# Fetching operand tiles as gathers by row number from a transposed table in DRAM

## Chip, cores and metric

The kernel runs on one core of a Trainium2 chip. The metric is the device time of one execution in microseconds (us); the median of three runs before is 1005.7 us.

## What is computed

A compressed interaction network over x of shape (1024, 39, 64), float32, in three layers with 64 outputs each. Each layer forms all products of its input's rows with the rows of x, and contracts them with a weight matrix:

```python
def _cin_layer(Xk, X0, W, b):
    O = W.shape[0]
    Hk, Fdim = (Xk.shape[1], X0.shape[1])
    Wr = W.reshape(O, Hk, Fdim)
    return jnp.einsum('bhe,bfe,ohf->boe', Xk, X0, Wr) + b[None, :, None]
X0 = sparse_embedding
Xk = X0
outs = []
for W, b in ((W0, b0), (W1, b1), (W2, b2)):
    Xk = _cin_layer(Xk, X0, W, b)
    outs.append(Xk.sum(axis=-1))
cin_output = jnp.concatenate(outs, axis=-1)
return cin_output @ fc_w.T + fc_b
```

## The kernel before

Only products x[f] * x[g] of two rows of x are needed: the last layer is folded into the weights, and the outputs of the first layer are multiplied with a second linear form of the same products. Every unordered pair (f, g) of the 39 rows (fields) is formed once. The 65536 columns (batch times 64) are worked off in 32 blocks of 2048 columns (BLK), so that one row of a block is 8 KB.

**Operand tiles.** For a block n, the tile r[n] holds four operands of 128 partitions by 2048 columns. Operand i holds 39 fields three times, each time rotated by a different amount (BASE, STEP), on 117 partitions, and 11 more rows (EXTRA) on the rest; operand 0 has ones there instead. The six pairs of operands (PAIRS) give six products of 128 rows (chunks 0 to 5). The seventh chunk holds what is left and needs only half of the partitions: the tiles u and v hold two blocks at once, the even one on partitions 0 to 63, the odd one on 64 to 127. There are two buffers of r (rt), two of u and two of v.

**How the tiles are filled.** load (L113) brings a block of x, transposed to fields by columns in pieces of 256 bytes, into an SBUF stage tile xs. store (L119) writes that twice into a DRAM tile xd of 78 rows, so that a rotation is one run of rows. roll (L124) then reads each operand back with one copy of 117 rows from xd (L127), and the 11 extra rows of operands 1 to 3 with one more (L128). roll_half (L132) fills the half tiles with five copies (L139). In the steady loop operands 0 and 1 are issued on SP's queue and 2 and 3 on POOL's; L128, store and roll_half are on SP's, load is on POOL's.

**The weights.** Before the loop, W0 and the folded W1, W2 are written into two DRAM tables (wide0, wide), and gathered (L227) in the row order of the chunks into wa and wb; POOL issues the gathers from wide0, ACT and SP those from wide. DVE adds wb to wa, one chunk at a time, in the first block (L356).

**The loop.** The order is written out by hand. steps lists (block, chunk); an even block has seven chunks, an odd one six. DVE forms the product of four steps ahead (product, L277 and L279) into one of four buffers p. TensorE multiplies it with wa (multiply, L294, and L305 for the half chunk), into two PSUM tiles a block. After the first chunk of a block, finish for the block before runs: ACT L325, DVE L329 and L333; and fields copies 39 rows of u (ACT L318). When the loop comes to chunk 0 of block n it issues roll(n+1), and then roll_half(n+2), store(n+3) and load(n+4).

Of the kernel before, what the change touches and what calls it, by code (L numbers as in the profile page):

```python
# [45 lines left out]

F32 = mybir.dt.float32  # L50
AF = mybir.ActivationFunctionType
ALU = mybir.AluOpType
AX = mybir.AxisListType

B, F, E, H = 1024, 39, 64, 64
FH = F * H
NG = 3
K = NG * F
STEP = (0, 15, 9, 6)
BASE = (0, 3, 5, 20)  # L60
LAST = 11
EXTRA = (None, 6, 17, 28)
NX = 11
HR = 64
# [5 lines left out]
BLK = 2048  # L70
BB = BLK // E
SB = SUB // E
NBLK = B // BB
FW = 2 * F
FX = FW + 2

_dist = sorted(
    min(d % F, -d % F)
# [9 lines left out]
def rows(t, first, steps, n):  # L88

    base = t[:]  # L90
    width = base.ap[-1][1] if len(base.ap) == 2 else n
    ap = [[s * width, k] for s, k in steps] + [[1, n]]
    return bass.AP(base.tensor, base.offset + first * width, ap)
# [3 lines left out]
def cin_kernel(ctx: ExitStack, tc: tile.TileContext, x, w0t, b0, w1, b1, w2, b2, fc_w, fc_b, out):  # L97
    nc = tc.nc
    PSUM = bass.MemoryType.PSUM
    DRAM = bass.MemoryType.DRAM  # L100

    const = ctx.enter_context(tc.tile_pool(name="const", bufs=1))
    dram = ctx.enter_context(tc.tile_pool(name="dram", bufs=1, space=DRAM))
    xds = ctx.enter_context(tc.tile_pool(name="xds", bufs=5, space=DRAM))
    stage = ctx.enter_context(tc.tile_pool(name="stage", bufs=3))
    prods = ctx.enter_context(tc.tile_pool(name="prods", bufs=4))
    psum = ctx.enter_context(tc.tile_pool(name="psum", bufs=4, space=PSUM))
    ctx.enter_context(tc.manual_schedule())

    xv = x.rearrange("b f e -> f b e")  # L110
    xs, xd, r = {}, {}, {}

    def load(n, engine):  # L113
        xs[n] = stage.tile([F, BLK], F32, name="xs", tag="xs")
        engine.dma_start(  # L115
            xs[n].rearrange("p (b e) -> p b e", e=E), xv[:, n * BB : (n + 1) * BB, :]
        )

    def store(n):  # L119
        xd[n] = xds.tile([FW, BLK], F32, name="xd", tag="xd")  # L120
        nc.sync.dma_start(xd[n][0:F], xs[n])
        nc.sync.dma_start(xd[n][F:FW], xs[n])

    def roll(n, engines):  # L124
        r[n] = rt[n % 2]
        for i in range(4):
            engines[i].dma_start(r[n][0:K, i], rows(xd[n], BASE[i], [(1, F), (STEP[i], NG)], BLK))  # L127
        nc.sync.dma_start(  # L128
            r[n][K:128, 1:4], rows(xd[n], EXTRA[1], [(1, NX), (LAST, 3)], BLK)
        )  # L130

    def roll_half(n):  # L132
        h = n % 2 * HR
        for t, pieces in (
            (ut, ((0, 56, 0), (56, 62, 28))),
            (vt, ((0, F, 0), (45, 56, 34), (56, 62, F))),
        ):
            for p0, p1, first in pieces:
                nc.sync.dma_start(  # L139
                    t[n // 2 % 2][h + p0 : h + p1], xd[n][first : first + p1 - p0]  # L140
                )

    wa = const.tile([128, NCHUNK, 2 * H], F32, name="wa")
    wb = const.tile([128, NCHUNK, 2 * H], F32, name="wb")
    fc = const.tile([H, 3], F32, name="fc")
    fc2 = const.tile([H, 32], F32, name="fc2")
    v2 = const.tile([H, FX], F32, name="v2")
    bias = const.tile([H, 2], F32, name="bias")
# [2 lines left out]
    wfin = const.tile([H + F, 1], F32, name="wfin")  # L151
    kfin = const.tile([1, 1], F32, name="kfin")

    rt = [const.tile([128, 4, BLK], F32, name=f"r{k}") for k in range(2)]
    ut = [const.tile([128, BLK], F32, name=f"u{k}") for k in range(2)]
    vt = [const.tile([128, BLK], F32, name=f"v{k}") for k in range(2)]
# [6 lines left out]
    prep = tc.tile_pool(name="prep", bufs=1)  # L163
    with prep as prep:

        w2s = prep.tile([H, FH], F32, name="w2s")
        w1s = prep.tile([H, FH], F32, name="w1s")
        nc.sync.dma_start(w2s, w2)
        nc.scalar.dma_start(fc, fc_w.rearrange("o (l h) -> h (o l)", h=H))
        nc.scalar.dma_start(w1s, w1)  # L170
        load(0, nc.sync)
        w0v = w0t.rearrange("b a h -> b (a h)")
        for i in range(2):
            for k in range(2):
                engine = nc.scalar if i else nc.gpsimd
                engine.dma_start(wide0v[i * F : (i + 1) * F, k * F * H : (k + 1) * F * H], w0v)
        nc.scalar.dma_start(bias[:, 0:1], b1.rearrange("(h o) -> h o", o=1))
        nc.scalar.dma_start(bias[:, 1:2], b2.rearrange("(h o) -> h o", o=1))
        nc.scalar.dma_start(b0s[H:128], b0.rearrange("(h o) -> h o", o=1))
        nc.scalar.dma_start(fcb, fc_b.rearrange("(p o) -> p o", o=1))  # L180
        for k in range(2):
            nc.gpsimd.memset(rt[k][96:128, 0], 1.0)
            nc.gpsimd.memset(ut[k], 1.0)
            nc.gpsimd.memset(vt[k], 1.0)
        store(0)
        roll(0, [nc.sync] * 4)
        roll_half(0)

        nc.vector.memset(wa, 0.0)
        nc.vector.memset(wb, 0.0)  # L190
        nc.vector.memset(wfin[0:H], 1.0)
        nc.vector.tensor_copy(fc2, fc[:, 2:3].to_broadcast([H, 32]))
        nc.vector.tensor_copy(v2[:, FW:FX], fc[:, 1:2].to_broadcast([H, 2]))  # L193


        n8 = 8 * F
        pv = psum.tile([128, 2, MM], F32, name="pv", tag="po")
        vrow = prep.tile([128, 2, n8], F32, name="vrow")
        for half in range(2):
            for t in range(4):  # L200
                g = 4 * half + t
                nc.tensor.matmul(  # L202
                    pv[32 * t : 32 * t + 32, half, 0:n8],
                    fc2,
                    w2s[:, g * n8 : (g + 1) * n8],
                    start=True,
                    stop=True,
                )
            nc.vector.tensor_copy(vrow[:, half], pv[:, half, 0:n8])
            nc.scalar.dma_start(v2[32 * half : 32 * half + 32, 0:F], vrow[0:128:32, half])  # L210
        nc.vector.tensor_copy(v2[:, F:FW], v2[:, 0:F])  # L211


        w1v = w1s.rearrange("o (h f) -> o f h", f=F)
        for g in range(5):
            f0, f1 = 8 * g, min(8 * g + 8, F)
            n = (f1 - f0) * H
            pt = psum.tile([128, SUB], F32, name="pt", tag="po")
            nc.tensor.matmul(pt[0:FX, :n], v2, w1v[:, f0:f1, :], start=True, stop=True)  # L219
            part = prep.tile([FX, MM], F32, name=f"part{g}")  # L220
            nc.vector.tensor_copy(part[:, :n], pt[0:FX, :n])  # L221
            for k in range(2):
                nc.scalar.dma_start(widev[:, (k * F + f0) * H : (k * F + f1) * H], part[:, :n])
# [23 lines left out]
        main(nc.gpsimd, wa[:, c], wide0, i, k, w0cols)  # L247
        main(nc.gpsimd, wb[:, c], wide0, k, i, w0cols)
    rest(nc.gpsimd, nc.gpsimd, wide0, w0cols)
    load(1, nc.gpsimd)  # L250
    load(2, nc.gpsimd)
    gather(nc.sync, wa[K:128, 0:3, tcols], wide, FW * FW + EXTRA[1], (1, NX), (LAST, 3))
    for c, (i, k) in enumerate(PAIRS):
        main(nc.scalar, wa[:, c], wide, i, k, tcols)
        main(nc.sync if c % 2 else nc.scalar, wb[:, c], wide, k, i, tcols)
    gather(nc.sync, wa[F:45, NPAIR, tcols], wide, FW * FW, (1, 6))
    rest(nc.sync, nc.scalar, wide, tcols)
    store(1)
    roll_half(1)


    pc = psum.tile([128, SUB], F32, name="pc", tag="po")
# [3 lines left out]
    nc.scalar.copy(wfin[H : H + F], pc[0:F, 0:1])  # L266
    nc.scalar.activation(kfin, pc[0:1, MM : MM + 1], AF.Identity, bias=fcb, scale=float(E))

# [52 lines left out]
    def finish(n):  # L321
        x1 = []
        for h in range(BLK // SUB):
            t = work.tile([H, SUB], F32, name="x1", tag="x1")
            nc.scalar.activation(t, po[n][h][H:128, :], AF.Identity, bias=b0s[H:128])  # L325
            x1.append(t)
# [14 lines left out]
    p = {s: product(*s) for s in steps[:AHEAD]}  # L341
    for at, (n, c) in enumerate(steps):
        if c == 0:
            if n + 1 < NBLK:
                roll(n + 1, [nc.sync, nc.sync, nc.gpsimd, nc.gpsimd])
            for k in (2, 3) if n == 0 else (n + 3,):
                if n > 0 and n + 2 < NBLK:
                    roll_half(n + 2)
                if k < NBLK:
                    store(k)  # L350
                if k + 1 < NBLK:
                    load(k + 1, nc.gpsimd)
            if n == 0:
                roll_half(2)
        if n == 0:
            nc.vector.tensor_tensor(wa[:, c], wa[:, c], wb[:, c], ALU.add)  # L356
            if c == NPAIR:
                nc.scalar.copy(wa[HR : 2 * HR, c], wa[0:HR, c])  # L358
        multiply(n, c, p.pop((n, c)))
        if c == 0:  # L360
            if n > 0:
                finish(n - 1)
            fields(n)
        if at + AHEAD < len(steps):
            p[steps[at + AHEAD]] = product(*steps[at + AHEAD])
# [3 lines left out]
    for m in range(B // MM):  # L369
        py = psum.tile([128, SUB], F32, name="py", tag="po")  # L370
        nc.tensor.matmul(py[0:1, 0:MM], wfin, sums[:, bass.ts(m, MM)], start=True, stop=True)  # L371
        nc.scalar.activation(y[:, bass.ts(m, MM)], py[0:1, 0:MM], AF.Identity, bias=kfin)
    nc.sync.dma_start(out.rearrange("b o -> o b"), y)
# [42 lines left out]
```

## Time and profile before

| what | value |
|---|---|
| runs before, us | 996.43, 1005.7, 1010.02 |
| profiled execution, us | 992.35 |
| its span from first to last instruction, us | 990.2 |
| DMA traffic, MB | 198.58 |
| HBM read, written, MB | 176.12, 23.61 |
| ACT busy, us | 141.1 |
| POOL busy, us | 90.4 |

The busy times are sums over the span, which holds a start (the weights, some 60 us), the loop, and an end. The DMA share is the mean busy share of the core's 16 DMA engines. Ends of matmuls are modelled in the trace, so a busy TensorE need not be at its full pace.

### The profile page before, as it was taken

The page shows a single profiled execution, that of the slowest core. Times are in us where ns is not written, and L with a number is a line of the kernel's source. Part 1 is how long each engine was busy: PE and PEld are TensorE (multiplying, and loading weights), DVE is VectorE, ACT ScalarE, POOL GpSimd, SP SyncE. Part 2 cuts the span into 40 slices and gives each one's busy share as a digit, 9 for nine tenths or more (in the row PEclk, how much of TensorE's full clock was granted, in tenths as well). Part 3 has the DMA queues.
Part 4 walks back from the last instruction along what each step waited for, and adds up shares of the span by engine and source line. Part 5 has one row for each costly group of instructions (what it writes and reads, how often), then busy time and mean ns, then how long its engine had stood idle before and what let it go on. Part 6 is the DMA issues. An engine that isn't in the chain of part 4 may idle for free.

```text
span 990.2 us, 5329 instructions
## 1 busy us (share of the span) xinstructions
PE 787.0 (79%) x1828; PEld 335.2 (34%) x1828; DVE 624.3 (63%) x356; ACT 141.1 (14%) x134; POOL 90.4 (9%) x124
## 2 busy tenths in 40 slices
PE   1334599789688799695978999786969969598997
PEld 0011244334233243242433434332424324243442
DVE  1151386587766485784765778765849577395794
ACT  0010021102111111010111021110211101021112
POOL 7210000000000000010000000000000000000000
PEclk9997799989898989797999899898988979799999
DMA  7749889889898889798888879888888988889830
GB/s 194 236 105 203 215 209 213 217 208 229 214 208 210 194 217 204 208 212 214 215 202 211 211 228 218 229 222 212 224 211 213 194 194 215 225 205 204 197 85 0
DMA packets 37658, 198.58 MB, mean 201 GB/s; under 512 B 11633, under 2 KB 11828, under 8 KB 15043
## 3 DMA queue, kind: packets, MB, share of 16 engines
q1 hardware_dynamic: 20633, 124.39, 50.8%
q0 software_dynamic: 14128, 70.55, 30.6%
q10 hardware_dynamic: 2870, 3.30, 1.1%
q8 instruction: 14, 0.23, 0.1%
q14 instruction: 13, 0.11, 0.0%
HBM read 176.12 MB, written 23.61 MB: 202 GB/s over the span
## 4 chain that ended last, share of the span: by engine, by line
DMA 86%; PE 7%; DVE 2%; SPq 1%; issue 1%; ACTq 1%; ACT 0%; DVEq 0%
DMA r<-xd 45%; DMA xd<-xs 18%; DMA u<-xd 18%; PE po L294 6%; DVE p L277 2%; DMA wide<-part 2%; DMA xs<-in_x 1%; DMA v<-vrow 1%; ACTq L227 1%; DMA wa<-wide 1%; SPq L227 0%; SPq L139 0%; PE po L305 0%; SPq L127 0%; DVE g L329 0%
## 5 line engine op out<-in xcount | busy, mean ns | idle before, releaser
L294 PE MATMUL po<-p,wa 128*128 128x512 f32 x1536 | 712.7, 626 | 172.3 <-DVE p L277 120.2
L277 DVE TENSOR_TENSOR p<-r 128x2048 f32<-128x2048 f32 x192 | 428.8, 2285 | 313.6 <-DMA r<-xd 238.8
L294 PEld LDWEIGHTS po<-p,wa 128*128 128x128 f32 x1536 | 306.3, 201 | 577.8 <-issue 410.4
L325 ACT ACTIVATE x<-po,b0s 64x1024 f32<-64x1024 f32 x64 | 71.1, 1111 | 349.5 <-PE po L305 194.9
L318 ACT COPY g<-u 39x1024 f32<-39x1024 f32 x64 | 66.6, 1043 | 377.1 <-DVE sums L333 377.1
L127 POOL DMA_DIRECT2D r<-xd x62 | 36.0, 581 | 828.7 <-DVE p L277 708.3
L329 DVE SCALAR_TENSOR_TENSOR g<-po,fc,x 64x1024 f32<-64x1024 f32 x64 | 81.2, 1269 | 8.4 <-ACT x L325 8.4
L333 DVE TENSOR_REDUCE sums<-g 103x16 f32<-103x1024 f32 x64 | 78.1, 1220 | 2.2
L305 PE MATMUL po<-p,wa 64*128 64x512 f32 x256 | 61.1, 615 | 2.6 <-DVE wa L356 2.6
L279 DVE TENSOR_TENSOR p<-u,v 128x2048 f32<-128x2048 f32 x16 | 36.6, 2284 | 8.2 <-DMA v<-xd 8.2
L305 PEld LDWEIGHTS po<-p,wa 64*128 64x128 f32 x256 | 25.8, 192 | 36.8 <-issue 32.4
L115 POOL DMA_DIRECT2D xs<-in_x x31 | 31.2, 1007 | 1.9 <-issue 1.6
L219 PE MATMUL pt<-w1s,v 64*80 64x512 f32 (+1 forms) x10 | 9.5, 1109 | 13.0 <-DVE v L211 13.0
L202 PE MATMUL pv<-w2s,fc 64*32 64x312 f32 x16 | 2.5, 724 | 8.6 <-DVE v L193 8.0
L358 ACT COPY wa<-wa 64x128 f32<-64x128 f32 x1 | 0.3, 296 | 61.9 <-DVE wa L356 61.9
L266 ACT ACT_TABLE_LOAD x1 | 1.3, 1283 | 54.3 <-DMA wb<-wide 54.3
L219 PEld LDWEIGHTS pt<-w1s,v 64*80 64x80 f32 x10 | 2.2, 230 | 19.8 <-DVE v L211 14.1
L211 DVE COPY v<-v 64x39 f32<-64x39 f32 x1 | 0.2, 176 | 12.2 <-DMA v<-vrow 12.2
L221 DVE COPY part<-pt 80x512 f32<-80x512 f32 (+1 forms) x5 | 3.4, 673 | 6.8 <-PE pt L219 6.8
L227 POOL DMA_DIRECT2D wa<-wide x10 | 6.5, 650 | 4.9 <-DMA wb<-wide 2.8
L227 POOL DMA_DIRECT2D wb<-wide x9 | 6.0, 672 | 2.2 <-DMA wb<-wide 2.2
L371 PE MATMUL py<-sums,wfin 103*1 103x512 f32 x4 | 2.2, 620 | 3.7 <-DVE sums L333 3.7
(26 smaller groups left out, 22.5 us busy)
## 6 DMA issues: line engine op xcount, KB each, us to landing
r<-xd SPq DMA_DIRECT2D x66, 936.0 KB
r<-xd POOLq DMA_DIRECT2D x62, 936.0 KB, 20.0
xd<-xs SPq DMA_DIRECT2D x64, 312.0 KB
u<-xd SPq DMA_DIRECT2D x32, 448.0 KB
v<-xd SPq DMA_DIRECT2D x32, 312.0 KB
xs<-in_x POOLq DMA_DIRECT2D x31, 312.0 KB, 25.7
r<-xd SPq DMA_DIRECT2D x32, 264.0 KB
v<-xd SPq DMA_DIRECT2D x32, 88.0 KB
```

The lines of the kernel that those rows point to most:

```text
L115: engine.dma_start(xs[n].rearrange("p (b e) -> p b e", e=E), xv[:, n * BB : (n + 1) * BB, :])
L127: engines[i].dma_start(r[n][0:K, i], rows(xd[n], BASE[i], [(1, F), (STEP[i], NG)], BLK))
L219: nc.tensor.matmul(pt[0:FX, :n], v2, w1v[:, f0:f1, :], start=True, stop=True)
L227: engine.dma_start(dst, rows(table, first, steps, H))
L277: nc.vector.tensor_tensor(p, r[n][:, i], r[n][:, k], ALU.mult)
L279: nc.vector.tensor_tensor(p, ut[n // 2 % 2], vt[n // 2 % 2], ALU.mult)
L294: nc.tensor.matmul(po[n][m // 2][:, at], wa[:, c, :], p[:, bass.ts(m, MM)], start=(c == 0 and first), stop=(c == NPAIR - 1 and not first),)
L305: nc.tensor.matmul(po[n + h][m // 2][:, at], wa[w, c, :], p[w, bass.ts(m, MM)], start=(h == 1), stop=(h == 0),)
L318: nc.scalar.copy(gt[H : H + F], ut[n // 2 % 2][h : h + F, bass.ts(m, SUB)])
L325: nc.scalar.activation(t, po[n][h][H:128, :], AF.Identity, bias=b0s[H:128])
L329: nc.vector.scalar_tensor_tensor(gt[0:H], po[n][h][0:H, :], fc[:, 0:1], x1[h], ALU.add, ALU.mult)
L333: nc.vector.tensor_reduce(sums[:, b_at : b_at + SB], gt.rearrange("p (b e) -> p b e", e=E), AX.X, ALU.add)
```

## The change

The stage tile, the DRAM tile of 78 rows and the copies of roll and roll_half go. Three DRAM tables of 80 rows of 8 KB (xd0 to xd2) hold two blocks each: rows 0 to 38 and 40 to 78 are the fields, rows 39 and 79 are ones. load writes a block of x into its table directly, from DRAM to DRAM, on SP's queue and four blocks ahead. Ten lists of 128 row numbers are made at the start by POOL (iota) and DVE, written to DRAM and read back transposed into an SBUF tile (lists, 128 by 10). Each operand tile is one indirect DMA on POOL's queue: 128 rows of 8 KB, row p taken from the table by the number in partition p of the list. A block needs four of them; u and v of a pair of blocks need one each. Copied rows include the ones and, in u and v, padding. The six memsets of rt, ut and vt go.

```diff
-    xds = ctx.enter_context(tc.tile_pool(name="xds", bufs=5, space=DRAM))
-    stage = ctx.enter_context(tc.tile_pool(name="stage", bufs=3))
...
+    xd = [dram.tile([2 * FT, BLK], F32, name=f"xd{k}") for k in range(NTAB)]
+
+    def load(n):
+        first = n % 2 * FT
+        nc.sync.dma_start(
+            xd[n // 2 % NTAB][first : first + F].rearrange("f (b e) -> f b e", e=E),
+            xv[:, n * BB : (n + 1) * BB, :],
         )
...
-    def roll(n, engines):
+    def gather_rows(dst, n, k):
+        table = xd[n // 2 % NTAB][: FT if k < 4 else 2 * FT]
+        nc.gpsimd.indirect_dma_start(
+            dst, None, table, bass.IndirectOffsetOnAxis(ap=lists[:, k : k + 1], axis=0)
+        )
+
+    def roll(n):
         r[n] = rt[n % 2]
         for i in range(4):
-            engines[i].dma_start(r[n][0:K, i], rows(xd[n], BASE[i], [(1, F), (STEP[i], NG)], BLK))
-        nc.sync.dma_start(
-            r[n][K:128, 1:4], rows(xd[n], EXTRA[1], [(1, NX), (LAST, 3)], BLK)
-        )
+            gather_rows(r[n][:, i], n, n % 2 * 4 + i)
 
     def roll_half(n):
...
+        gather_rows(ut[n // 2 % 2], n, 8)
+        gather_rows(vt[n // 2 % 2], n, 9)
...
+        nc.vector.memset(row, 0)
+        for i in range(4):
+            nc.gpsimd.iota(
+                row[:, i, 0:K], pattern=[[1, F], [STEP[i], NG]], base=BASE[i], channel_multiplier=0
+            )
+            if i:
+                ramp(i, K, NX, EXTRA[i])
...
+        nc.vector.tensor_scalar(wrap, row, F, -F, ALU.is_ge, ALU.mult)
+        nc.vector.tensor_tensor(row, row, wrap, ALU.add)
...
+        ones = prep.tile([2, BLK], F32, name="ones")
+        nc.vector.memset(ones, 1.0)
...
-        load(0, nc.sync)
+        load(0)
+        nc.sync.dma_start(rowd, row)
+        nc.sync.dma_start(lists, rowd.rearrange("k p -> p k"), allow_slow_non_contiguous=True)
+        for k in range(NTAB):
+            nc.sync.dma_start(xd[k][F : 2 * FT : FT], ones)
+        load(1)
...
-        for k in range(2):
-            nc.gpsimd.memset(rt[k][96:128, 0], 1.0)
-            nc.gpsimd.memset(ut[k], 1.0)
-            nc.gpsimd.memset(vt[k], 1.0)
-        store(0)
-        roll(0, [nc.sync] * 4)
-        roll_half(0)
+        roll(0)
...
     rest(nc.gpsimd, nc.gpsimd, wide0, w0cols)
-    load(1, nc.gpsimd)
-    load(2, nc.gpsimd)
+    roll_half(0)
...
     rest(nc.sync, nc.scalar, wide, tcols)
-    store(1)
-    roll_half(1)
+    load(2)
+    load(3)
...
             if n + 1 < NBLK:
-                roll(n + 1, [nc.sync, nc.sync, nc.gpsimd, nc.gpsimd])
-            for k in (2, 3) if n == 0 else (n + 3,):
-                if n > 0 and n + 2 < NBLK:
-                    roll_half(n + 2)
-                if k < NBLK:
-                    store(k)
-                if k + 1 < NBLK:
-                    load(k + 1, nc.gpsimd)
-            if n == 0:
-                roll_half(2)
+                roll(n + 1)
+                if n % 2:
+                    roll_half(n + 1)
+            if n + 4 < NBLK:
+                load(n + 4)
```

## Rows read from the trace of the kernel before

**Rows 1.** The page: span; engines' busy us, share of the span, instructions.

```profile
span 990.2 us, 5329 instructions
PE 787.0 (79%) x1828; PEld 335.2 (34%) x1828; DVE 624.3 (63%) x356; ACT 141.1 (14%) x134; POOL 90.4 (9%) x124
```

**Rows 2.** The page's 40 slices: granted TensorE clock and DMA busy share, in tenths.

```profile
PEclk9997799989898989797999899898988979799999
DMA  7749889889898889798888879888888988889830
```

**Rows 3.** The page's chain that ended last, share of the span by line.

```profile
DMA r<-xd 45%; DMA xd<-xs 18%; DMA u<-xd 18%; PE po L294 6%; DVE p L277 2%; DMA wide<-part 2%; DMA xs<-in_x 1%; DMA v<-vrow 1%; ACTq L227 1%; DMA wa<-wide 1%; SPq L227 0%; SPq L139 0%; PE po L305 0%; SPq L127 0%; DVE g L329 0%
```

**Rows 4.** Waits: engine line <- releaser: us in total, times, longest us.

```profile
DVE p L277 <- DMA r<-xd: 238.8, 25, 19.0
...
PE po L294 <- DVE p L277: 120.2, 21, 11.5
...
SPq L122 <- DMA r<-xd: 183.4, 28, 11.6
```

**Rows 5.** DMA issues: out<-in, queue, xcount, KB each, median us to landing.

```profile
r<-xd SPq DMA_DIRECT2D x66, 936.0 KB
r<-xd POOLq DMA_DIRECT2D x62, 936.0 KB, 20.0
xd<-xs SPq DMA_DIRECT2D x64, 312.0 KB
u<-xd SPq DMA_DIRECT2D x32, 448.0 KB
v<-xd SPq DMA_DIRECT2D x32, 312.0 KB
xs<-in_x POOLq DMA_DIRECT2D x31, 312.0 KB, 25.7
```

**Rows 6.** Windows: stretch, length, busy us (x) by engine, PEclk, DMA share, GB/s.

```profile
2.00:5.00 3.00, 0.00 (x0) 0.00 (x0) 0.74 (x2) 0.00 (x0) 2.90 (x3) 1.00 0.99 210
...
22.00:24.00 2.00, 0.00 (x0) 0.00 (x0) 0.09 (x1) 0.00 (x0) 0.79 (x2) 1.00 0.66 245
24.00:26.00 2.00, 1.86 (x2) 0.57 (x3) 0.08 (x1) 0.00 (x0) 2.00 (x4) 1.00 0.94 294
...
110.00:880.00 770.00, 647.84 (x1520) 279.55 (x1519) 519.02 (x286) 116.62 (x109) 57.35 (x80) 0.92 0.88 212
```

**Rows 7.** Timeline of TensorE at the end: start us, us, engine, line, operation, xcount.

```profile
956.93 3.70 PE L305 MATMUL po<-p,wa 64*128 64x512 f32 x16
960.57 20.87 PE L294 MATMUL po<-p,wa 128*128 128x512 f32 x48
```

**Rows 8.** Timeline of DVE at the end, one odd block.

```profile
954.39 8.90 DVE L277 TENSOR_TENSOR p<-r 128x2048 f32<-128x2048 f32 x4 [0.41 <-DMA r<-xd]
963.20 1.27 DVE L329 SCALAR_TENSOR_TENSOR g<-po,fc,x 64x1024 f32<-64x1024 f32 x1
...
968.08 4.48 DVE L277 TENSOR_TENSOR p<-r 128x2048 f32<-128x2048 f32 x2
```

**Rows 9.** Views of tiles r and xs: ns min/median/max, first and last start.

```profile
L277 DVE TENSOR_TENSOR p<-r x192: 2280/2284/2294, 49.5 to 970.3; 128x2048 f32<-128x2048 f32 x192
L127 POOL DMA_DIRECT2D r<-xd x62: 572/583/631, 70.9 to 928.7; - x62
...
L115 POOL DMA_DIRECT2D xs<-in_x x31: 986/1006/1042, 32.0 to 842.3; - x31
```

**Rows 10.** Timeline of the start, lines that bear on the first matmul.

```profile
20.07 18.62 SPq L127 DMA_DIRECT2D r<-xd  x4
...
44.75 0.87 ACTq L227 DMA_DIRECT2D wa<-wide  x1
...
58.93 0.29 SPq L227 DMA_DIRECT2D wa<-wide  x1
...
60.94 5.82 PE L294 MATMUL po<-p,wa 128*128 128x512 f32 x8 [26.92 <-DVE wa L356]
```

More of the change, by code (lines that the diff above doesn't have):

```diff
@@ L50 @@
 F32 = mybir.dt.float32
+I32 = mybir.dt.int32
 AF = mybir.ActivationFunctionType
@@ L75 @@
 FX = FW + 2
+FT = F + 1
+NTAB = 3
 _dist = sorted(
@@ L110, in cin_kernel @@
     xv = x.rearrange("b f e -> f b e")
[L111 to L116, printed above, removed]
-        )
[L119 to L122, printed above, removed]
-    def roll(n, engines):
+    r = {}
+    xd = [dram.tile([2 * FT, BLK], F32, name=f"xd{k}") for k in range(NTAB)]
[4 more added lines that the diff above has]
+            xv[:, n * BB : (n + 1) * BB, :],
+        )
+    def gather_rows(dst, n, k):
[4 more added lines that the diff above has]
+    def roll(n):
         r[n] = rt[n % 2]
         for i in range(4):
-            engines[i].dma_start(r[n][0:K, i], rows(xd[n], BASE[i], [(1, F), (STEP[i], NG)], BLK))
-        nc.sync.dma_start(
-            r[n][K:128, 1:4], rows(xd[n], EXTRA[1], [(1, NX), (LAST, 3)], BLK)
-        )
+            gather_rows(r[n][:, i], n, n % 2 * 4 + i)
     def roll_half(n):
[L133 to L141, printed above, removed]
+        gather_rows(ut[n // 2 % 2], n, 8)
+        gather_rows(vt[n // 2 % 2], n, 9)
     wa = const.tile([128, NCHUNK, 2 * H], F32, name="wa")
@@ L152, in cin_kernel @@
     kfin = const.tile([1, 1], F32, name="kfin")
+    lists = const.tile([128, 10], I32, name="lists")
     rt = [const.tile([128, 4, BLK], F32, name=f"r{k}") for k in range(2)]
@@ L164, in cin_kernel, with ramp @@
     with prep as prep:
+        row = prep.tile([1, 10, 128], I32, name="row")
+        wrap = prep.tile([1, 10, 128], I32, name="wrap")
+        rowd = dram.tile([10, 128], I32, name="rowd")
+        def ramp(k, first, n, start):
+            nc.gpsimd.iota(row[:, k, first : first + n], pattern=[[1, n]], base=start, channel_multiplier=0)
+        nc.vector.memset(row, 0)
[5 more added lines that the diff above has]
+                ramp(i, K, NX, EXTRA[i])
+        ramp(8, 0, 56, 0)
+        ramp(8, 56, 6, 28)
+        ramp(9, 0, F, 0)
+        ramp(9, 45, 11, 34)
+        ramp(9, 56, 6, F)
+        nc.vector.tensor_scalar(wrap, row, F, -F, ALU.is_ge, ALU.mult)
+        nc.vector.tensor_tensor(row, row, wrap, ALU.add)
+        for k, first, end in ((0, K, 128), (8, 62, HR), (9, F, 45), (9, 62, HR)):
+            nc.vector.memset(row[:, k, first:end], F)
+        nc.vector.tensor_scalar(row[:, 4:8], row[:, 0:4], FT, None, ALU.add)
+        nc.vector.tensor_scalar(row[:, 8:10, HR:128], row[:, 8:10, 0:HR], FT, None, ALU.add)
         w2s = prep.tile([H, FH], F32, name="w2s")
         w1s = prep.tile([H, FH], F32, name="w1s")
+        ones = prep.tile([2, BLK], F32, name="ones")
+        nc.vector.memset(ones, 1.0)
         nc.sync.dma_start(w2s, w2)
```

## The prediction

> **What bounds the kernel now.** I read the busy times first: TensorE is busy for 787 us of 990.2, DVE for 624 [rows 1]. Neither fills the span. The slices come next: the DMA engines stand at eight or nine tenths from the second eighth of the span to its end, while the granted clock of TensorE dips to seven tenths again and again, as it does when TensorE has stood still [rows 2]. The chain settles it: r<-xd, xd<-xs and u<-xd together are 81% of the span, matmuls 6% [rows 3]. The waits say who pays: DVE stood 238.8 us before a product because an operand had not landed, and TensorE 120.2 us because a product was not there [rows 4]. So each block is bound by the filling of its tiles.
>
> How fast is that filling? The loop's stretch from 110 to 880 us holds 1520 of the 1536 + 256 matmuls, thus 1520 / 1792 x 32 = 27.1 blocks, or 28.4 us a block, at 212 GB/s with the DMA engines 0.88 busy [rows 6]. That is 28.4 x 212 = 6.02 MB a block. Two things are to be seen in it. First, many of these bytes are not operands: the block is stored twice (2 x 312 KB) after it was loaded (312 KB) [rows 5]. Second, the engines are busy but slow. In the stretch 24 to 26 us, where the rolls of block 0 run almost alone, a share of 0.94 moved 294 GB/s, or 313 with all engines busy, and just before a share of 0.66 moved 245; in the stretch 2 to 5 us the load of W2 to 64 partitions held them 0.99 busy for 210; in the loop a full share would be 212 / 0.88 = 241 [rows 6]. A transfer that touches few partitions keeps the engines busy and moves little; u (448 KB, 56 rows), v (312 KB, 39 rows) and the stores out of 39 partitions are of that kind [rows 5].
>
> [...]
>
> There is also a queue in it: SP waited 183.4 us at the second store for an earlier roll [rows 4], and everything behind it on SP, the next rolls of operands 0 and 1 among it, stood in line.
>
> **The change, part by part.**
>
> *Bytes.* A block's four gathers carry 4 x 128 x 8 KB = 4.19 MB, its half of u and v 1.05 MB, the load 0.32 MB: 5.56 MB in place of 6.02. By the loop's present rate that takes 5.56 / 212 = 26.2 us a block, with all engines busy at their present speed (241) 23.1 us, and by the stretch of lone rolls (313) 17.8 us. The gathers are all of 128 partitions, come one after the other on one queue, and no store or narrow copy is left between them; so they are nearest to the lone rolls. I take 18 to 23 us a block and keep 26.2 as the upper end.
>
> *The load from DRAM to DRAM.* Its 1248 pieces of 256 bytes are now short on the writing side too. No row shows that. The nearest is the present load, which lands 25.7 us after its issue in the crowd [rows 5]. It is issued four blocks before its gathers, so even twice this is hidden by some 68 us of matmuls (three blocks of 22.7, below); uncovered it would cost those 25.7 us once a block. Its engine time is within the rates above. SP has nothing else in the loop, so nothing queues behind it.
>
> *Gathers on POOL.* Five a block, issued in order. No row shows an indirect DMA. The direct ones take POOL 0.58 us for 117 rows and 1.01 us for the load's pieces [rows 9]; below, five of 0.58 are 2.9 us a block; above, with each held up by one whole product of 2.28 us as well, 5 x (1.01 + 2.28) = 16.5 us, still under TensorE's 22.7. I take about 1 us each, hidden. What queues behind a waiting gather: operand 1 of block n+1 waits for the last product of block n-1, and behind it stand operands 2 and 3 and, every second block, u and v. From that last product to the first product of block n+1 lie seven or eight steps of 3.5 us of matmul (8 of 0.434 us), some 25 us. The first product needs two gathers: at 1.05 MB / 212 GB/s = 4.9 us each they land in some 10 us. So the double buffer is enough.
>
> *What is then late.* TensorE. At the end of the trace, with no transfers left, 48 matmuls take 20.87 us and the 16 of the half chunk 3.64 (956.93 to 960.57), without a gap [rows 7]. [...] DVE in that stretch: products 2.22 us apart, 13 a pair, and 4.9 us of finish a block (963.20 to 968.08) [rows 8]: 13 x 2.22 + 9.8 = 38.7 us a pair, under 45.4. So 16 x 45.4 = 726 us of matmuls, if the tiles come in 22.7 us a block.
>
> *The start.* The first matmul is at 60.94 us, behind an addition that waits for gathered weights; SP's own gathers of weights came only at 58.93 since they stood behind roll and roll_half of block 0, although ACT's began at 44.75 [rows 10]. That queue is now free, a gain of up to 14 us, bounded by ACT's gathers (some 10 us of issue and a landing), so 4 to 6. Against it, DVE makes lists before it starts on W2; the six POOL memsets go and fifteen iotas come. No row has iotas; between nothing and the memset's length the lists cost the weights 0 to 10 us, and I take 3. The roll of block 0 was issued at 20.07 [rows 10]; with lists, ones and table it will be much the same, and it is not what the first matmul waits for. I take the first matmul at 57 us, with 50 and 68 as ends. Then block 1 is ready early, where now the second block's tiles are late.
>
> *The sum.* 57 + 726 + 9 (from the last matmul, 960.57 + 20.87 = 981.4, to 990.2) = 792; 6 for the first matmuls at half clock (8 took 5.82 us where 3.5 is the full pace [rows 10]) and single stalls; 2 from the span to the profiled execution's time: 800 us against 992.35. The median of the runs lies 1.35% above the profiled one, so 810.
>
> **The rivals.**
>
> *Transfers stay the bound.* If the gathers run at the loop's 212 GB/s, a block takes 26.2 us; from about 20 us on, 32 x 26.2 = 838, and some 30 for the last block and the end: 890, 902 by the median. For it speaks that 212 is the only rate seen for long; against it, the lone rolls at 294.
>
> *POOL and DVE hold each other up.* A gather reads its list out of SBUF, which no DMA of POOL does now; today neither side is stretched (products 2280 to 2294 ns, POOL's copies 572 to 631) [rows 9]. If a product and a list's reading exclude each other, ten gathers a pair lengthen DVE's 38.7 us. It decides from (45.4 - 38.7) / 10 = 0.67 us a gather; at 1.01 us a pair is 48.8 us, the sum 16 x 48.8 + 57 + 9 + 8 = 855, by the median 866. [...]
>
> [...]
>
> *Nothing moves.* The double buffer or a slow load could leave a block at 28 to 29 us. It needs just under 6 us a gather; little speaks for it.
>
> **How the numbers follow.** TensorE the bound, 785 to 840: 0.58. Transfers still the bound, 840 to 960: 0.15. Lock, 840 to 900: 0.09. No change (within 2%, about what a measurement here can tell from none): 0.05. Slower: 0.13. So faster 0.82, same 0.05, slower 0.13. The range 780 to 940 holds the first case, the lock and most of the second; the likeliest alone would be 785 to 840.
>
> **What would show it.** Right: PE over 90% busy, the chain made of L294, the clock at full in nearly all slices, waits of products on r<-xd near nothing, DMA share well under 0.88, gathers of POOL about 1 us. [...]

## The result

The changed kernel takes 798.28 us (four runs, 797.51 to 800.19) against 1001.07 for the kernel before: a ratio of 0.797, interval 0.790 to 0.804. The prediction was 810, within 780 to 940.

The page of the changed kernel, its head, engines and slices, to be read beside [rows 1, 2]:

```profile
span 796.2 us, 4955 instructions
...
PE 742.2 (93%) x1828; PEld 320.2 (40%) x1828; DVE 635.6 (80%) x366; ACT 141.1 (18%) x134; POOL 264.8 (33%) x197
...
PEclk9999999999999999999999999999999999999998
DMA  6979566565667766565677756565676755555400
```

TensorE is busy for 93% of the span, its granted clock is 1.00 through the whole loop (95 to 760 us; 0.89 on the mean of 64 to 95 us, in the first block, where TensorE stood still for 2.6 us ahead of each chunk), and the DMA engines have time to spare (a share of 0.63, below). In the kernel before, the six slices with a clock of seven tenths [rows 2] are slices in which TensorE was busy for four to six tenths (the first three, at one to three tenths, had nine):

```profile
PE   1334599789688799695978999786969969598997
```

The chain by line, in shares of the span, has changed hands [rows 3]:

```profile
PE po L317 83%; PE po L328 8%; DMA r<-xd,lists 2%; DMA rowd<-row 1%; DMA u<-xd,lists 1%; POOL wb L251 0%; POOL wa L251 0%; POOL r L125 0%; DVE g L352 0%; DVE sums L356 0%; DMA xd<-ones 0%; PE py L389 0%; DVE wa L374 0%; POOL row L171 0%; DVE row L182 0%
```

L317 and L328 are the matmuls (L294 and L305 before), L300 a product. DVE's products now wait for TensorE to free a buffer and hardly for a transfer; of the 238.8 us behind r [rows 4] 3.7 are left, in the start. Waits, in us in total, times, longest us:

```profile
DVE p L300 <- PE po L317: 90.5, 66, 5.3
```

And one stretch of the loop, with the columns of [rows 6]: TensorE has no idle time in it, the DMA share is 0.63.

```profile
185.00:760.00 575.00, 575.00 (x1426) 250.73 (x1425) 497.23 (x270) 109.81 (x102) 197.82 (x123) 1.00 0.63 238
```

### The profile page after: what moved, and what is told of

It reads as the page before. It is cut to its first block, busy times and chain, and to the rows that moved or that the text cites. A ratio compares the mean times of both kernels' runs of the same rounds, so it can differ in the third digit from the quotient of the medians.

```text
span 796.2 us, 4955 instructions
## 1 busy us (share of the span) xinstructions
PE 742.2 (93%) x1828; PEld 320.2 (40%) x1828; DVE 635.6 (80%) x366; ACT 141.1 (18%) x134; POOL 264.8 (33%) x197
## 4 chain that ended last, share of the span: by engine, by line
PE 91%; DMA 4%; issue 2%; POOL 2%; DVE 1%; ACT 0%; DVEq 0%; SPq 0%; POOLq 0%; ACTq 0%
PE po L317 83%; PE po L328 8%; DMA r<-xd,lists 2%; DMA rowd<-row 1%; DMA u<-xd,lists 1%; POOL wb L251 0%; POOL wa L251 0%; POOL r L125 0%; DVE g L352 0%; DVE sums L356 0%; DMA xd<-ones 0%; PE py L389 0%; DVE wa L374 0%; POOL row L171 0%; DVE row L182 0%
## 5 line engine op out<-in xcount | busy, mean ns | idle before, releaser
L317 PE MATMUL po<-p,wa 128*128 128x512 f32 x1536 | 668.1, 596 | 28.9 <-DVE wa L374 28.9
L300 DVE TENSOR_TENSOR p<-r 128x2048 f32<-128x2048 f32 x192 | 435.8, 2290 | 121.9 <-PE po L317 90.5
L317 PEld LDWEIGHTS po<-p,wa 128*128 128x128 f32 x1536 | 291.3, 191 | 403.8 <-issue 367.1
L125 POOL DMA_INDIRECT r<-xd,lists x128 | 204.0, 1593 | 454.1 <-DVE p L300 383.4
L328 PE MATMUL po<-p,wa 64*128 64x512 f32 x256 | 61.0, 615 | 2.6 <-DVE wa L374 2.6
L328 PEld LDWEIGHTS po<-p,wa 64*128 64x128 f32 x256 | 25.8, 191 | 36.8 <-issue 33.1
L125 POOL DMA_INDIRECT u<-xd,lists x16 | 30.4, 1900 | 4.9 <-issue 4.9
L125 POOL DMA_INDIRECT v<-xd,lists x16 | 15.1, 941 | 4.9 <-issue 4.9
```

Of the source, the lines that this page charges most:

```text
L125: nc.gpsimd.indirect_dma_start(dst, None, table, bass.IndirectOffsetOnAxis(ap=lists[:, k : k + 1], axis=0))
L300: nc.vector.tensor_tensor(p, r[n][:, i], r[n][:, k], ALU.mult)
L317: nc.tensor.matmul(po[n][m // 2][:, at], wa[:, c, :], p[:, bass.ts(m, MM)], start=(c == 0 and first), stop=(c == NPAIR - 1 and not first),)
L328: nc.tensor.matmul(po[n + h][m // 2][:, at], wa[w, c, :], p[w, bass.ts(m, MM)], start=(h == 1), stop=(h == 0),)
```

## Experiments

All are edits of the changed kernel, but for before_half_work. Those on one chip share runs of the kernel before, which lay between 996.57 and 1011.74 us. Each experiment is one run, adds_ahead four.

**Which part of the change it was.** Three kernels keep the table in DRAM and the load from x into it four blocks ahead, with the fields twice in the table, and go back to copies for all tiles, for r alone, or for u and v alone.

```diff
-FT = F + 1
+FT = FW + 1
...
-            gather_rows(r[n][:, i], n, n % 2 * 4 + i)
+            engine.dma_start(
+                r[n][0:K, i], rows(table, first + BASE[i], [(1, F), (STEP[i], NG)], BLK)
+            )
+        nc.sync.dma_start(
+            r[n][K:128, 1:4], rows(table, first + EXTRA[1], [(1, NX), (LAST, 3)], BLK)
+        )
...
-        gather_rows(ut[n // 2 % 2], n, 8)
-        gather_rows(vt[n // 2 % 2], n, 9)
+                    nc.sync.dma_start(
+                        t[n // 2 % 2][h + p0 : h + p1],
+                        xd[n // 2 % NTAB][at + first : at + first + p1 - p0],
+                    )
```

all_copied has both edits, rolls_copied the first, half_copied the second.

> The table in DRAM and its load four blocks ahead are kept (with the fields twice in it, so that a rotation is one run of rows), but every operand tile is filled by the copies of the kernel before. Theory 1 (the shape and mixture of the copies made them slow): the transfers stay the bound at 212 to 241 GB/s, 5.7 MB are 24 to 27 us a block, 840 to 920 us, products wait for r. Theory 2 (the stores and the line on SP's queue made them slow): TensorE is the bound as in the changed kernel, 795 to 810 us.

Measured: 994.39 us, beside 997.73 for the kernel before. A stretch of its loop, and waits of DVE and of SP's queue (L150 are the copies to u and v):

```profile
110.00:700.00 590.00, 498.47 (x1193) 216.64 (x1194) 406.64 (x225) 90.79 (x85) 24.07 (x42) 0.92 0.86 201
```

```profile
DVE p L321 <- DMA r<-xd: 266.3, 16, 35.0
...
SPq L150 <- DMA r<-xd: 171.6, 48, 14.1
```

A block is 56 matmul records, so 1193 are 21.3 blocks, 27.7 us each where it was 28.4. Both theories miss in size, and theory 2 falls as far as the stores go: without a single store, and with the table loaded far ahead, nearly nothing is gained, though a second load from x stands in the stores' place. The line on SP's queue is still there (SP waited 171.6 us for rolls, where it was 183.4 at the second store [rows 4]), so this run does not test it. Theory 1 was too mild: the rate did not rise either, it fell to 201 GB/s.

> As all_copied, but u and v are gathered as in the changed kernel; only the four operands of r are copied in 117 and 11 rows. Theory 1: a block carries 4.1 MB by copies and 1.05 MB by gathers; if the narrow copies of u and v were the worst part it comes to 800 to 840 us, if the copies of 117 rows are slow by themselves to 840 to 900. Theory 2: 795 to 810 us.

Measured: 913.15 us, a little over the range of the slow copies of 117 rows.

```profile
110.00:700.00 590.00, 538.02 (x1305) 234.24 (x1306) 441.16 (x244) 101.62 (x95) 78.15 (x68) 0.96 0.90 224
```

That is 23.3 blocks, 25.3 us each. Gathering u and v took 81 us off, gathering r another 115. So filling r by copies is slow with no copies to u and v beside it; the 11 extra rows are still a narrow copy of their own here (264 KB), which gathers_117 below does without.

> The changed kernel with all arithmetic, r gathered in 128 rows, u and v filled by the narrow copies of the kernel before. Copied r with gathered u and v took 913 us, all copied 994. If the costs add as bytes at a rate: 4.19 MB at 402 GB/s and 0.97 MB of narrow copies and the loads at 200 are 10.4 + 8 = 18.4 us, under TensorE's 22.6: 795 to 805 us. If narrow copies beside a gather slow the gather to their own rate: 5.8 MB at 230 GB/s are 25 us, 850 to 890 us.

Measured: 835.08 us, between the two, and for another reason than either. The loop is at TensorE's pace:

```profile
130.00:780.00 650.00, 650.00 (x1614) 283.25 (x1614) 560.85 (x304) 124.80 (x116) 190.43 (x115) 1.00 0.82 251
```

The 37 us are lost ahead of the first matmul. Timeline of the start, SP's queue and TensorE:

```profile
38.48 10.25 SPq L120 DMA_DIRECT2D xd<-in_x  x2
...
65.21 0.30 SPq L265 DMA_DIRECT2D wa<-wide  x1
...
80.99 5.56 PE L331 MATMUL po<-p,wa 128*128 128x512 f32 x8 [39.54 <-DVE wa L388]
```

SP's gathers of weights (L265) stand behind the narrow copies of blocks 0 and 1 again, and behind the load of block 1 (L120), which is doubled in this kernel. The first matmul comes at 80.99 where the changed kernel has it at 44.32. So in the loop the copies of u and v are hidden once r is quick, and what is lost is lost at the start; how much of that is the narrow copies' alone is not shown, as the doubled load and a slower making of the lists (last section) are in it too. Taken in this order, gathering r is worth 159 us and gathering u and v the last 37.

**What makes a transfer quick.** half_rows splits every gather by partitions, half_cols by columns.

```diff
-            dst, None, table, bass.IndirectOffsetOnAxis(ap=lists[:, k : k + 1], axis=0)
+        for h, numbers in enumerate((lists, upper)):
+            at = bass.IndirectOffsetOnAxis(ap=numbers[0:64, k : k + 1], axis=0)
+            nc.gpsimd.indirect_dma_start(dst[64 * h : 64 * h + 64], None, table, at)
```

```diff
+        table = table.rearrange("p (c n) -> (p c) n", n=SUB)
+        for h in range(2):
+            at = bass.IndirectOffsetOnAxis(ap=lists2[:, h, k : k + 1], axis=0)
+            nc.gpsimd.indirect_dma_start(dst[:, bass.ts(h, SUB)], None, table, at)
```

> Each gather is split into two of 64 rows, partitions 0 to 63 and 64 to 127: same bytes, twice the gathers. [...] If the number of partitions of a transfer does not matter: 795 to 810 us, DMA share 0.6 to 0.7 in the loop. If POOL's time is what matters, half_cols shows the same.

> Each gather is split into two of 1024 columns over all 128 partitions: same bytes and as many gathers as half_rows, rows of 4 KB. Theory 1: 795 to 810 us, DMA share 0.6 to 0.7, unlike half_rows. If the count of gathers (POOL's time, held up by products) is what matters: 10 gathers a block of 1 to 2.75 us reach 22.7 us, and it is slower, 820 to 900 us, as half_rows would be.

Measured: half_rows 835.19 us, half_cols 804.0. The same stretch of each, half_rows first:

```profile
110.00:700.00 590.00, 569.39 (x1399) 244.96 (x1398) 480.74 (x262) 107.65 (x100) 495.03 (x243) 1.00 1.02 231
```

```profile
110.00:700.00 590.00, 590.00 (x1468) 257.05 (x1467) 508.53 (x276) 112.00 (x104) 448.20 (x262) 1.00 0.73 245
```

Same bytes, same number of gathers. (A share of 1 or a little over stands for engines busy without a pause.) Over half of the partitions the DMA engines are busy all the time for 231 GB/s, and TensorE waits for them; over all partitions in half rows they are busy 0.73 of it for 245. So what counts here is how many rows, and with them partitions, one transfer covers; the number of gathers and POOL's time do not. With 5.24 MB at the 210 GB/s that the load of W2 to 64 partitions had [rows 6], half_rows would have needed 25 us a block, 850 to 900 us in all, which was my estimate; a block took 23.6 us (1399 matmuls are 25.0 blocks).

Then the transfers laid bare: only the arithmetic of half of the columns, so that TensorE is no longer the bound.

```diff
-            nc.vector.tensor_tensor(p, r[n][:, i], r[n][:, k], ALU.mult)
+            nc.vector.tensor_tensor(p[:, :SUB], r[n][:, i, :SUB], r[n][:, k, :SUB], ALU.mult)
...
-        for m in range(BLK // MM):
+        for m in range(SUB // MM):
```

> The changed kernel with all transfers, but products, matmuls and sums of the first 1024 columns of each block only; the rest of the arithmetic is left out. TensorE's part of a block falls to 11.4 us, so the transfers are bare. Theory 1: 14 to 18 us a block (0.63 of 22.5 us were busy; 5.56 MB at 313 GB/s are 17.8), 500 to 630 us. If gathers carry no more than the loop before did (212 GB/s): 26 us a block, 850 to 890 us.

> The kernel before with all transfers, but the arithmetic of the first 1024 columns of each block only; the rest is left out. If the transfers alone set the 28.4 us a block: 940 to 1010 us, as with all the work. If the turn of products, buffers and queues had a part in it: 850 to 930 us or less.

Measured: 502.97 and 963.28 us. One stretch of each, after_half_work first; a block has 28 matmul records here:

```profile
110.00:450.00 340.00, 296.85 (x692) 117.39 (x692) 245.00 (x209) 52.00 (x49) 164.85 (x121) 0.98 1.01 402
```

```profile
110.00:450.00 340.00, 164.57 (x349) 68.05 (x348) 118.11 (x103) 28.27 (x27) 26.10 (x36) 0.74 0.89 214
```

The gathers need 13.8 us a block (692 / 28 = 24.7 blocks) at 402 GB/s; the kernel before needs 27.3 us with half of the arithmetic as well as 28.4 with all of it. So its transfers, with their queues, set its pace, and the change halves them.

Last, rows and form apart: gathers of 117 rows, and plain copies of 128.

```diff
-            gather_rows(r[n][:, i], n, n % 2 * 4 + i)
+            gather_rows(r[n][0:K, i], n, n % 2 * 4 + i)
```

```diff
-            gather_rows(r[n][:, i], n, n % 2 * 4 + i)
+        for i, engine in enumerate([nc.sync, nc.sync, nc.gpsimd, nc.gpsimd]):
+            engine.dma_start(r[n][:, i], xd[n // 2 % NTAB][BASE[i] : BASE[i] + 128])
```

copies_128_pool has nc.gpsimd in all places.

> The changed kernel with the arithmetic of the first 1024 columns only (the rest is left out, as in after_half_work: 501 us, 402 GB/s), and the operands of r gathered in 117 rows in place of 128; the other 11 rows are not fetched. 5.20 MB a block. If the number of rows (how 117 of them fall on 16 engines and on the partitions) made the copies slow: 5.20 MB at 212 to 250 GB/s, 21 to 25 us a block, 700 to 840 us. If the gather's way of issuing is what is fast: 5.20 MB at 402 GB/s, 13 us, 460 to 490 us.

> As after_half_work (arithmetic of the first 1024 columns only), but each operand tile is one straight copy of 128 rows that lie one behind the other in the table (not the operand's rows), for r on SP's and POOL's queues, two and two, for u and v on SP's. 5.9 MB a block, with the fields twice in the table. If 128 rows at a time are what matters: 5.9 MB at 400 GB/s are 14.7 us, 500 to 560 us. If two queues side by side or copies as such are slow: 700 to 900 us.

> As copies_128 with all copies on POOL's queue, one after the other as the gathers are. If only 128 rows matter: 500 to 560 us, as copies_128. If the mixing of queues is the loss: 500 to 560 here and 600 or more there.

Measured: gathers_117 795.48 us, copies_128 564.28, copies_128_pool 562.45, the last two a little over their 500 to 560. The same stretch, in this order:

```profile
110.00:450.00 340.00, 223.50 (x421) 82.34 (x420) 150.87 (x127) 33.35 (x31) 95.22 (x70) 0.81 1.02 227
```

```profile
110.00:450.00 340.00, 277.36 (x635) 114.97 (x633) 219.39 (x189) 48.22 (x45) 23.10 (x44) 0.91 1.01 377
```

```profile
110.00:450.00 340.00, 274.04 (x615) 102.72 (x614) 216.48 (x184) 47.38 (x44) 54.01 (x103) 0.98 0.98 377
```

Eleven rows fewer in each operand of r, and the same stretch falls from 402 to 227 GB/s; the run takes 293 us more. Plain copies of 128 rows run at 377, on one queue or on two, with the load doubled beside them. So in these rates a gather has no great advantage over a copy; what it adds is that it can bring 117 rotated rows and 11 others in as one transfer of 128.

The DMA packets in the traces, from 150 to 450 us, say what "slow" is here. A row of 8 KB took 309 ns in the median in after_half_work and in copies_128, but 565 in gathers_117, 575 in half_rows and 527 in the kernel before. In the first four, 15 to 17 such rows were under way at once for three quarters of the time or more. So the DMA engines are not short of work: with 117 or 64 rows to a transfer, each row takes longer.

**Do POOL and DVE hold each other up?** half_products cuts each product of r in two.

```diff
-            nc.vector.tensor_tensor(p, r[n][:, i], r[n][:, k], ALU.mult)
+            for m in range(2):
+                at = bass.ts(m, SUB)
+                nc.vector.tensor_tensor(p[:, at], r[n][:, i, at], r[n][:, k, at], ALU.mult)
```

> The products of r are formed in two operations of 1024 columns each. If a gather is held until the product that runs ends (0.81 us after it in the changed kernel): no gather takes longer than 0.81 + 1.15 + some 0.3, thus 2.3 us, where 28 took 2.7. If the long gathers wait for something else, such as room for their descriptors: up to 2.75 us as now. The time stays 795 to 815 us in either case.

Measured: 797.07 us, but gathers of up to 5.09 us, which neither case had. First the changed kernel, timeline of POOL and DVE:

```profile
417.64 2.75 POOL L125 DMA_INDIRECT r<-xd,lists  x1 [12.00 <-DVE p L300]
...
412.89 9.10 DVE L300 TENSOR_TENSOR p<-r 128x2048 f32<-128x2048 f32 x4
```

Then half_products:

```profile
416.86 5.08 POOL L125 DMA_INDIRECT r<-xd,lists  x1 [11.20 <-DVE p L302]
...
411.97 9.16 DVE L302 TENSOR_TENSOR p<-r 128x1024 f32<-128x1024 f32 x8
```

In the changed kernel the gather ends at 420.39, 0.7 us after the third of four products that stand back to back (412.89 + 9.10 x 3/4 = 419.7). In half_products it ends at 421.94, which is 0.81 us after the last of eight (411.97 + 9.16 = 421.13): it was held through three boundaries. So a product does hold a gather up, as was expected, but my rule that it is held until the running product ends is wrong; why it came in between full products and not between halves is open. No run shows a cost in time.

**The first block.** The page of the changed kernel has 28.9 us of TensorE behind L374, the addition of the weights (more of it below). adds_ahead issues that addition one chunk ahead.

```diff
         if n == 0:
-            nc.vector.tensor_tensor(wa[:, c], wa[:, c], wb[:, c], ALU.add)
+            for k in range(0 if c == 0 else c + 1, min(c + 2, NCHUNK)):
+                nc.vector.tensor_tensor(wa[:, k], wa[:, k], wb[:, k], ALU.add)
```

> In the first block the addition of wb to wa for a chunk is issued one chunk ahead, before the product that waits for a buffer p. If the 6.3 us a chunk there come from the order of DVE's queue (product, addition, matmuls one after the other): TensorE runs through the first block at 3.5 us a chunk, 16 to 20 us less, 776 to 784 us. If the gathers of the weights set that pace: 793 to 800 us.

Measured: 777.22 us (775.77 to 777.76), a ratio of 0.777 to the kernel before, interval 0.773 to 0.781: faster than both. TensorE's first row of the loop:

```profile
42.21 22.39 PE L317 MATMUL po<-p,wa 128*128 128x512 f32 x48 [14.17 <-DMA wa<-wide]
```

Six chunks without a gap. The order of DVE's queue was what set the pace, not the weights.

## Why the prediction came out right, step by step

**The bound before.** Right: with half of the arithmetic the kernel before takes 963 us.

**What made its transfers slow.** Partly wrong. Transfers to 64 partitions do hold the engines and move little: half_rows shows it by itself, 231 GB/s at a share of 1.02. The 210 at 0.99 of [rows 6], which I put down to W2, was not clean evidence, as W1, the first load and the copies of W0 were under way in the same stretch. And I took the copies of 117 rows for quick ones slowed by their company, as they moved 294 GB/s at the start. They are slow without it: 227 GB/s in gathers_117, where every other tile is a full gather. (At the start the rolls went on, from 35 to 40 us, at 267 GB/s with a share of 1.01; why that is more than 227 is open.) The two stores, to which I gave a part, have next to none: all_copied is 3 us quicker than the kernel before, within the spread of that kernel. The line on SP's queue no run takes away alone; gathers_117, with nothing but loads on SP in the loop, is slow without it. Why 64 rows are slow (231 GB/s where 128 have 402), and why 117 fare like 64, is open too: the engines are not idle (a share of 1.02 in both), but which engine writes which rows no trace shows.

**The transfers after.** The term was mis-sized: 18 to 23 us a block, where 13.8 are needed bare. The upper rate among my rows, 313 GB/s, was that of 117 rows. It cost nothing, as TensorE's 22.7 us cover it.

**TensorE's pace.** Right: a pair of blocks takes 41.40 + 3.63 = 45.03 us in the chain, against 45.4 (2 x 20.87 + 3.64) summed from [rows 7].

**The start and the first block.** Two terms were wrong, and it was luck that they cancelled. The first gathers of weights on SP and ACT in the changed kernel (start us, us), TensorE in its first block, and DVE:

```profile
39.46 0.32 SPq L251 DMA_DIRECT2D wa<-wide  x1
39.88 0.87 ACTq L251 DMA_DIRECT2D wa<-wide  x1
...
44.32 5.17 PE L317 MATMUL po<-p,wa 128*128 128x512 f32 x8 [15.93 <-DVE wa L374]
52.08 3.70 PE L317 MATMUL po<-p,wa 128*128 128x512 f32 x8 [2.59 <-DVE wa L374]
58.36 3.70 PE L317 MATMUL po<-p,wa 128*128 128x512 f32 x8 [2.58 <-DVE wa L374]
```

```profile
55.82 2.29 DVE L300 TENSOR_TENSOR p<-r 128x2048 f32<-128x2048 f32 x1 [3.79 <-PE po L317]
58.03 0.28 DVE L374 TENSOR_TENSOR wa<-wa,wb 128x128 f32<-128x128 f32 x1
```

The first matmul came at 44.32 where I had 57: with roll and its copies gone from SP's queue SP's gathers began 19 us sooner and ACT's 5, and the first matmul came 17 us sooner than at 60.94 [rows 10]. I had it wait for all of ACT's gathers, some 10 us of issue; it waited for those of its own chunk, and began 4.4 us after the first of them was issued. (The lists are twelve iotas, not fifteen, and W2's first matmul came at 11.95 in place of 8.00 us, near the 3 us that I took.) But a chunk of the first block then took 6.3 us in place of 3.5, two of them 7.8: a product waits for the buffer that the matmuls of the last chunk free, and the addition for the next chunk stands behind that product on DVE. The block ends at 90.5, 46.2 us after its start where a bare one takes 24.5, so 22 us more, for which I had 6. The half clock in that 6 the trace does not show at the first matmuls: the clock is given as 1.00 there, for the eight that took 5.82 us before [rows 10] (60.94 to 66.76 us) as for the eight that take 5.17 here (44.32 to 49.49). Where eight took 5.25 us, from 64.65 to 69.90, it was 0.70. The kernel before had the same stall, in a row of its waits that I passed over (us in total, times, longest us):

```profile
PE po L294 <- DVE wa L356: 52.2, 6, 26.9
```

Of that, 26.9 us lie ahead of the first matmul [rows 10], and 5.4 and 12.1 at two chunks whose products waited for late tiles (v and r); where no tile was late it was 2.6 us a chunk, as after the change. With the tiles on time the stall stands on the path by itself, and adds_ahead is 21 us quicker. Summed anew: 44.3 + 46.2 + the 31 blocks to 786.8 (696.3) + 9.4 to the end + 1.9 = 798.1. The last step of the forecast, 10 us for a median 1.35% above the profiled run, did not come either: the profiled run took 798.05 and the median is 798.28.

**The rivals.** Transfers as the bound: no, by the bare 13.8 us. Slower, by slow gathers (0.13): of 128 rows they are the quickest of the transfers compared (402 GB/s in after_half_work), though gathers_117 (227) and half_rows (231) show that a gather of fewer rows does lose its rate; by what mechanism is not shown. POOL and DVE holding each other up (the lock): it is there, on one side. Views of tile r in the changed kernel, ns min/median/max, beside [rows 9]:

```profile
L300 DVE TENSOR_TENSOR p<-r x192: 2279/2291/2312, 30.8 to 775.3; 128x2048 f32<-128x2048 f32 x192
L125 POOL DMA_INDIRECT r<-xd,lists x128: 937/942/2749, 19.4 to 738.3; - x128
```

A gather takes 0.94 us when nothing holds it and up to 2.75 beside products (of all gathers, the 74 that began beside a product took over 1.2 us); a product takes 7 ns more than before, four in a row 9.10 us for 8.90 [rows 8]. I had priced the lock at a full gather on DVE; it is paid by POOL, which has time (busy for 33% of the span). Not every operation of DVE holds a gather up: in after_half_work one passes in 0.94 us beside a sum (so do 24 of the 25 that began beside a sum or the operation ahead of it). What in a product makes the difference no run shows.

```profile
332.75 0.94 POOL L125 DMA_INDIRECT r<-xd,lists  x1 [0.30 <-DVE g L353]
...
332.74 1.22 DVE L357 TENSOR_REDUCE sums<-g 103x16 f32<-103x1024 f32 x1
```

## What to carry to other kernels

Divide the GB/s of a stretch by its DMA share before you count bytes: engines that are busy all the time at 231 GB/s, as in half_rows, may be moving the wrong shape. Here transfers of 128 rows carried 402 where those of 117 carried 227 and those of 64 carried 231. If a tile can't be one run of 128 rows, a gather by row numbers can make it one; pad it to 128 rather than leave rows out. And when a stall of the loop goes, look for the waits of the start that stood in its shadow, and list each wait of the bound engine, not only the longest.

## What the runs showed of the hardware that was not expected

In half_copied, which sets u and v on POOL at the start as the kernel before did, DVE's small operation on the lists takes 8.90 us; in the changed kernel, without the memsets, 0.81. POOL and DVE, start us and us:

```profile
5.89 1.84 POOL L223 MEMSET u<- 128x2048 f32 x1
...
11.12 1.84 POOL L224 MEMSET v<- 128x2048 f32 x1
...
4.74 8.90 DVE L192 TENSOR_SCALAR wrap<-row 1x1280 int32<-1x1280 int32 x1 [2.54 <-POOL row L178]
```

The same operation in the changed kernel:

```profile
4.74 0.81 DVE L181 TENSOR_SCALAR wrap<-row 1x1280 int32<-1x1280 int32 x1 [2.54 <-POOL row L167]
```

In half_copied it ends at 13.64, 0.7 us after the last of four memsets that follow one another. That looks as if the memsets had held it, and would be 8 of the 37 us of that kernel's late start; but by the records it began before the first memset, so there this is argued and not shown. gathers_117, which sets r on POOL in two memsets of some 7 us, has the two side by side:

```profile
6.28 14.07 POOL L212 MEMSET r<- 32x8192 f32 x2
...
7.23 6.24 DVE L185 TENSOR_SCALAR row<-row 1x512 int32<-1x512 int32 x1
13.40 7.02 DVE L186 TENSOR_SCALAR row<-row 1x128 int32<-1x128 int32 x1
```

The two operations take 0.41 and 0.21 us in the changed kernel. Here each ends just after the memset beside it (13.47 after 13.20, 20.42 after 20.34). That the memset on POOL holds the operation of DVE is how I read this; no run changed the memsets alone.

Pieces of 256 bytes from DRAM to DRAM were a small burden: with them among its transfers after_half_work moved 402 GB/s. In its packets such a piece took 18 ns, 14 bytes a ns where a row of 8 KB has 26.5, and all of them 0.09 of the engines' time.
